# The first image normed within the attention, loads and output tail moved, and a reordered MLP, in an attention and Fourier mixer kernel

## The chip, the cores and the metric

The kernel runs on one core of a Trainium2 chip. The core has a matrix engine (TensorE, PE in the profile; its weight loads are PEld), three engines for elementwise work (VectorE or DVE, ScalarE or ACT, GpSimd or POOL), a sync engine (SP) that issues DMAs here, and 16 DMA engines. Each engine works through its own instructions in order, so an instruction that waits holds up all behind it on that engine. The metric is device time in microseconds (us); lower is better. Since there is one core, its span is the time, but for a little around it.

## What is computed

Eight images of 128 x 128 positions and 64 channels, float32, go through two layers. The first is an attention of every position over its own column (H) and its own row (W), with one softmax over both. The second is a Fourier mixer block: layer norm, expansion to 128 channels, a 2D Fourier transform, a matrix over real and imaginary parts with GELU, the inverse transform, projection back; then a convolutional MLP. Cut to what matters:

```python
def _L0_conv_ref(x, w_q, b_q, w_k, b_k, w_v, b_v, gamma):
    ...
    att = jax.nn.softmax(jnp.concatenate([energy_H, energy_W], axis=-1), axis=-1)
    att_H, att_W = (att[..., :H], att[..., H:])
    out_H = jnp.einsum('bhwk,bkwc->bhwc', att_H, V)
    out_W = jnp.einsum('bhwv,bhvc->bhwc', att_W, V)
    return gamma[0] * (out_H + out_W) + x
...
    h = _pw(_ln(x, g1, b1), w_te, b_te)
    F = jnp.fft.fft2(h.astype(jnp.complex64), axes=(1, 2))
    fr = jnp.concatenate([jnp.real(F), jnp.imag(F)], axis=-1)
    fc = jax.nn.gelu(_pw(fr, w_fc, b_fc), approximate=False)
    re, im = (fc[..., :HID], fc[..., HID:])
    sp = jnp.real(jnp.fft.ifft2(re + 1j * im, axes=(1, 2)))
    x1 = x + _pw(sp, w_tp, b_tp)
    h2 = _pw(_ln(x1, g2, b2), w_fe, b_fe)
    d = lax.conv_general_dilated(h2, w_dw, window_strides=(1, 1), padding='SAME', dimension_numbers=('NHWC', 'HWIO', 'NHWC'), feature_group_count=HID) + b_dw
    d = jax.nn.gelu(d, approximate=False)
    return x1 + _pw(d, w_fp, b_fp)
```

## The kernel before

The program has two halves. All eight images pass the attention, whose result x2 is written to DRAM (one tensor for each image); then all eight pass the mixer, which reads x2 back.

**The attention** (lines 91 to 448) runs each image in 16 slots: n = 0 to 7 attend over H, n = 8 to 15 over W. The order on PE, DVE, ACT and POOL is the order of the code. A slot makes scores (e, L217), maxima (L226), exponentials (L258), for H a masking of the diagonal on POOL (L260), and the sums with the values. In the W slots from n = 10 on, and in two trailing slots, finish(o, r) makes an eighth of the output: POOL adds the bias to the input (xb, L327, twice), DVE forms the sum of the denominators (L336, from sumh, which was loaded back from DRAM) and scales (yo, L349), POOL adds both (yo, L354, twice), SP stores to x2 (L356), and DVE takes the statistics for the next layer norm (L366); after the last of them the reciprocal deviation goes to scale1. While an image is in its slots, the next one is loaded and transposed (xT, in a pool with one large buffer). During the last image's W slots there is no next image.

**The mixer** (lines 451 to 965) first prepares its constants (weights folded with norms, the tables of the transform), then takes one image after the other. Only PE's order is that of the code here. DVE, ACT, POOL and SP are ordered by a scheduler, which goes by its own estimate of when each instruction can run.

- load_norm(b), L576 to L600, reads x2 in 16 chunks of four row pairs (h, 128 - h): one DMA of 128 KB (L584) and four of 32 KB (L587), a multiplication by the deviation (L588), sum and difference of the pair into xn (L593, L594). The first chunk has a copy (L596) and a small matmul for row 64 (qp, L598). DVE does this for image 0, POOL for the others.
- fourier(b), L605 to L703, has three stages. W: 256 matmuls over one axis (aps, L614, copied by ACT at L615). K, the frequency stage: 19 steps, each with the other axis (fps, L630), the 256 x 256 matrix (fcps, L650), GELU (L655, ACT), sums on POOL (L658 to L668) and a projection (gps, L686). I: the inverse over both axes (yps, L708; dps, L717), and DVE adds the result to x1, which is two loaded halves of x2 (x, L722).
- mlp(b), L731 to L937, takes the finished x1 in 16 chunks of eight rows: statistics (L743, DVE), normed rows (xc, L750, POOL), transposition (tpn, L765 on PE; xtn, L768 on ACT; for some chunks row 0 of xtn is a copy on POOL, L762), and then either of two ways to the 3 x 3 convolution. Most chunks expand to 128 channels (hp, L789; h, L793) and take nine taps on ACT and DVE (acc, L839, L841), then GELU (L849). The chunks in on_pe (5 and 10; for the last image 1, 3, 5 to 13) do expansion and taps as matmuls (pc, L804, L808, L815). At the end POOL adds the bias to x1 (ot, L859), PE shrinks to 64 channels (op, L864), DVE adds (L868), SP stores (L869). tpn, hp, pc and op share two PSUM buffers; ot has two buffers as well. An iteration (k, e) of the loop handles a chunk k with taps and, in some of the iterations, a chunk e with matmuls; the order of the e iteration is: transpositions, convolved(e), expand of the next k, shrink.

The main loop (L947 to L965) weaves mlp(b - 1) into fourier(b): mlp is cut into 79 pieces by its yields, and after each step of fourier as many pieces are issued as keep their share at 1.04 times the share of fourier's work that is done (weights: W 1.0 a step, K 6.3, I 1.8). load_norm(b + 1) is taken into the I stage. After fourier(b) the remaining pieces are issued, and only then the next image. After image 7 its mlp runs alone.

Some of the lines:

```python
                    while share < 1.04 * pieces * done / work:
                        next(before, None)
                        share += 1
                    if step == I_STEP and done > work - I_STEP * 18.5:
                        next(after, None)
```

## Time and profile before

| | |
|---|---|
| median of 4 runs | 3625.1 us (3609.41 to 3628.69) |
| the profiled execution | 3609.96 us, span 3608.2 us |
| mean granted clock of TensorE | 0.905 of full |
| end of the attention's last addition (L354) | 1279.6 us |
| first matmul of image 0 in the mixer (L614) | 1349.7 us |
| first L614 of images 1 to 7 | 1531.8, 1797.8, 2071.5, 2335.3, 2608.0, 2879.4, 3150.5 us |
| last dps (L717) of image 7 | 3406.9 us |
| image 0: W, K, I stage | 18.2, 115.6, 48.4 us (no MLP beside it) |
| image 4: W, K, I stage | 19.6, 194.6, 58.4 us |

The stages' lengths are the distances between the first matmuls of L614, L630 and L708. A window of the trace gives for each engine its busy time in that stretch with its number of instructions, then TensorE's mean granted clock, the mean busy share of the DMA engines, and GB/s. A group has the line of the code, the engine, the operation, its operands and shape, its count, then busy time, the mean of one in ns, and the idle time just ahead of such instructions with what ended it. The chain of waits follows the work that ended last: start, length, what; "issue" is a stretch in which nothing on the engine explains the wait, and SPq and POOLq are the queues of SP and POOL. In the slices each digit is the busy share of a fortieth of the span in tenths.

### The profile page before, as it was taken

To read this page: it belongs to the slowest core of one execution; us is meant where nothing else is said; L and a number is where in the kernel's file an instruction comes from. 1 tells how busy PE (TensorE), PEld (TensorE's weight loads), DVE (VectorE), ACT (ScalarE), POOL (GpSimd) and SP (SyncE) were. 2 spreads that over 40 slices of the span, in tenths; PEclk is the share of its full clock that TensorE was granted. 3 is DMA by queue.
4 is the path that set the end of the run, shared out by engine and by line. 5 is a ranking of instruction groups with operands and counts; after the bars stand their busy time and mean duration, and the time that the engine had idled before them with its cause. 6 is when DMAs were issued, how large, how long until landed. Compare 5 with 4: busy or idle time off the path is not lost.

```text
span 3608.2 us, 77249 instructions
## 1 busy us (share of the span) xinstructions
PE 3176.5 (88%) x30612; PEld 2185.1 (61%) x30612; DVE 2293.7 (64%) x5373; ACT 1781.9 (49%) x2861; POOL 1815.7 (50%) x2148
## 2 busy tenths in 40 slices
PE   7989899898998929799899899799899799899697
PEld 4666666666666716566656556556656556656455
DVE  3565565756657560266776776776776776776865
ACT  3535445354453306365465476465465365466332
POOL 0233332433324416856755766756756755756221
PEclk8989999999999859899898899998899898999886
DMA  4434344353443250101301301301301301301011
GB/s 107 125 87 126 91 127 117 102 130 103 120 112 99 75 163 1 44 13 44 89 9 44 86 11 45 89 12 41 89 12 42 89 9 44 83 12 45 16 21 27
DMA packets 579068, 243.66 MB, mean 68 GB/s; under 512 B 490770, under 2 KB 576146, under 8 KB 576658
## 3 DMA queue, kind: packets, MB, share of 16 engines
q1 hardware_dynamic: 578706, 238.72, 25.5%
q8 instruction: 242, 3.96, 0.5%
q14 instruction: 120, 0.98, 0.1%
HBM read 169.92 MB, written 67.63 MB: 66 GB/s over the span
## 4 chain that ended last, share of the span: by engine, by line
PE 47%; ACT 8%; DVE 6%; POOL 5%; issue 4%; DMA 3%; SPq 2%; POOLq 0%; ACTq 0%; DVEq 0%
PE fcps L650 11%; PE gps L686 6%; PE op L864 6%; PE hp L789 4%; PE pc L804 3%; PE fps L630 3%; DMA xl<-x 2%; PE e L217 2%; DVE acc L841 2%; SPq L587 2%; PE pc L815 2%; DVE stats L743 2%; PE aps L614 2%; ACT gl L655 1%; PE dps L717 1%
## 5 line engine op out<-in xcount | busy, mean ns | idle before, releaser
L841 DVE SCALAR_TENSOR_TENSOR acc<-h,wdw,acc 128x512 f32<-128x512 f32 (+2 forms) x1776 | 1194.1, 730 | 207.2 <-ACT acc L839 194.3
L658 POOL TENSOR_TENSOR gl<-gl 128x512 f32<-128x512 f32 (+2 forms) x272 | 332.0, 1224 | 370.5 <-ACT gl L655 369.7
L655 ACT ACTIVATE gl<-fcps,bfc 128x512 f32<-128x512 f32 (+2 forms) x544 | 359.7, 672 | 122.4 <-PE fcps L650 106.7
L354 POOL TENSOR_TENSOR yo<-yo,xb 128x512 f32<-128x512 f32 x128 | 161.1, 1280 | 422.4 <-issue 272.4
L258 ACT ACTIVATE att<-e 128x1024 f32<-128x1024 f32 x256 | 248.3, 1022 | 240.6 <-PE e L217 240.5
L864 PEld LDWEIGHTS op<-wfp,gd 128*128 128x128 f32 x2048 | 284.2, 219 | 124.9 <-ACT gd L849 53.2
L864 PE MATMUL op<-wfp,gd 128*128 128x64 f32 x2048 | 293.0, 303 | 71.4 <-ACT gd L849 50.1
L260 POOL TENSOR_SCALAR_AFFINE_SELECT att<-att 128x1024 f32<-128x1024 f32 x128 | 136.9, 1094 | 400.1 <-ACT att L258 400.1
L868 DVE TENSOR_TENSOR ot<-op,ot 128x512 f32<-128x512 f32 (+2 forms) x136 | 89.5, 658 | 364.1 <-PE op L864 216.4
L650 PE MATMUL fcps<-f,wplus 128*128 128x512 f32 (+2 forms) x544 | 292.9, 621 | 26.7 <-ACT gl L655 25.6
L650 PE MATMUL fcps<-f,wminus 128*128 128x512 f32 (+2 forms) x544 | 280.3, 597 | 1.7 <-ACT gl L655 1.7
L686 PEld LDWEIGHTS gps<-wtp,gl 128*128 128x128 f32 x2016 | 255.8, 205 | 29.5 <-issue 21.0
L686 PE MATMUL gps<-wtp,gl 128*128 128x64 f32 x2016 | 264.5, 288 | 1.9 <-POOL gl L668 1.9
L859 POOL TENSOR_TENSOR ot<-x,bfp 128x512 f32<-128x512 f32 (+2 forms) x144 | 164.9, 1151 | 162.8 <-DMA out_dram<-ot 136.0
L217 PE MATMUL e<-qkH 8*128 8x128 f32 (+1 forms) x4096 | 196.4, 310 | 54.0 <-DVE negH L226 50.1
L217 PEld LDWEIGHTS e<-qkH 8*128 8x128 f32 (+1 forms) x4096 | 160.2, 207 | 117.8 <-DVE negH L226 60.5
L217 PEld LDWEIGHTS e<-qkW 8*128 8x128 f32 (+1 forms) x4096 | 138.8, 191 | 125.1 <-DVE negW L226 37.2
L722 DVE TENSOR_TENSOR x<-dps,x 128x256 f32<-128x256 f32 x256 | 100.7, 416 | 174.9 <-PE dps L717 174.5
L750 POOL TENSOR_TENSOR xc<-x,scale 128x512 f32<-128x512 f32 x128 | 132.5, 1045 | 148.2 <-PE tpn L765 106.0
L717 PE MATMUL dps<-ys,tb 128*128 128x512 f32 x256 | 152.2, 686 | 58.7 <-DVE x L722 58.0
L226 DVE TENSOR_REDUCE negH<-e 128x8 f32<-128x1024 f32 x128 | 149.9, 1213 | 78.7 <-PE e L217 78.7
L217 PE MATMUL e<-qkW 8*128 8x128 f32 (+1 forms) x4096 | 169.0, 290 | 27.4 <-DVE negH L226 17.4
(167 smaller groups left out, 6198.1 us busy)
## 6 DMA issues: line engine op xcount, KB each, us to landing
xl<-in_x_dram SPq DMA_DIRECT2D x256, 128.0 KB
xh<-in_x_dram SPq DMA_DIRECT2D x64, 512.0 KB
xw<-in_x_dram SPq DMA_DIRECT2D x256, 128.0 KB
x<-yo SPq DMA_DIRECT2D x256, 128.0 KB
x<-x SPq DMA_DIRECT2D x16, 2048.0 KB
out_dram<-ot SPq DMA_DIRECT2D x120, 256.0 KB
xl<-x SPq DMA_DIRECT2D x128, 128.0 KB
xl<-x SPq DMA_DIRECT2D x512, 32.0 KB
```

The costliest lines, as they stand in the source:

```text
L217: nc.tensor.matmul(es[q // 2][:, q % 2, i, :], lhsT=qk[part, lhs, 4 * (r % 2) + i, :], rhs=qk[part, rhs, 4 * (r % 2) + i, :], start=True, ...
L226: nc.vector.tensor_reduce(view[:, 2 * g : 2 * g + 2, 4 * r : 4 * r + 4], e, AX.X, ALU.max, negate=True)
L258: nc.scalar.activation(att, e.rearrange("p q i w -> p (q i) w"), AF.Exp)
L354: nc.gpsimd.tensor_tensor(flat, flat, xbs[g], ALU.add)
L650: nc.tensor.matmul(ps[:, 0:n], lhsT=w[:, cols], rhs=fv, start=True, stop=not mean)
L655: nc.scalar.activation(gl[:, half, sgn, 0:n], ps[:, 0:n], AF.Gelu, bias=bfc[:, half : half + 1])
L658: nc.gpsimd.tensor_tensor(gl[:, half, 1, 0:n], gl[:, half, 0, 0:n], gl[:, half, 1, 0:n], ALU.add if half == 0 else ALU.subtract,)
L686: nc.tensor.matmul(gps[:, j, t, :], lhsT=src[:, j * P : j * P + P], rhs=wtp, start=True, stop=True)
L717: nc.tensor.matmul(dps.rearrange("p c h -> p (c h)"), lhsT=idw, rhs=ys.rearrange("p c h -> p (c h)"), start=True, stop=True)
L841: nc.vector.scalar_tensor_tensor(out=av, in0=src, scalar=wdw[:, t : t + 1], in1=av, op0=ALU.mult, op1=ALU.add)
L859: nc.gpsimd.tensor_tensor(ot[:, o : o + m, :], rows, bfp.unsqueeze(1).to_broadcast([P, m, C]), ALU.add)
L864: nc.tensor.matmul(op[:, i, :], lhsT=gls[k][:, i0 + a + i, :], rhs=wfp, start=True, stop=True)
```

## The change

Six edits. (1) Image 0 is loaded, scaled and folded beside the last image's attention: in each of its W slots SP issues the loads of eight row pairs (one of 256 KB and eight of 32 KB) and POOL does the scaling, the sum and the difference, at the end of the slot, into a buffer that outlives the attention; the row for the small matmul is kept, and the matmul stands at the mixer's end of preparation. (2) The large buffers of the mixer alternate between this outer pool and its own, one each instead of two in one pool. (3) The two x1 halves are requested at steps 10 and 17 of K rather than after K. (4) The factor 1.04 becomes 1.0; what is left of an MLP after its image's fourier is carried into the next image's steps, one piece after every fourth, and the end of the MLP is cut into more pieces. (5) In iterations with an e, expand stands ahead of convolved. (6) The MLP after the last image takes the statistics of 24 rows, the first norming, then those of the other 40.

```diff
+X1_AT = (10, 17)
...
+def folded(eng, xl, xn, scale, j):
+    n = xl.shape[2]
+    eng.tensor_tensor(xl, xl, scale[:, :, j : j + n].unsqueeze(3).to_broadcast([P, 2, n, C]), ALU.mult)
+    i = 0 if j else 1
+    one, two = (xl[:, s, i:, :].rearrange("p h c -> p c h") for s in range(2))
+    eng.tensor_tensor(xn[:, :, j + i : j + n], one, two, ALU.add)
+    eng.tensor_tensor(xn[:, :, 64 + j + i : 64 + j + n], one, two, ALU.subtract)
+    if j == 0:
+        eng.tensor_copy(xn[:, :, 0], xl[:, 0, 0, :])
+def load_pairs(nc, xl, img, j):
+    n = xl.shape[2]
+    nc.sync.dma_start(out=xl[:, 0, :, :], in_=img[:, j : j + n, :])
+    for i in range(n):
+        h = P - j - i if j + i else 64
+        nc.sync.dma_start(out=xl[:, 1, i, :], in_=img[:, h, :])
...
-                o.xT = big.tile([P, 64, P], F32, tag="xt", name="xt")
+                o.xT = one.tile([P, 64, P], F32, tag="xt", name="xt")
...
+            if cur and not nxt and n >= R:
+                j = 8 * (n - R)
+                if n == R:
+                    cur.xn = one.tile([P, C, P], F32, tag="xt", name="xn")
+                pairs = rows.tile([P, 2, 8, C], F32, tag="xl", name="xl", bufs=2)
+                load_pairs(nc, pairs, x2[0], j)
+                folded(nc.gpsimd, pairs, cur.xn, scale1[:, 0, :].rearrange("p (s j) -> p s j", s=2), j)
+                if j == 0:
+                    nc.gpsimd.tensor_copy(row64, pairs[:, 1, 0, :])
...
-        big = ctx.enter_context(tc.tile_pool(name="m_big", bufs=2))
+        big = ctx.enter_context(tc.tile_pool(name="m_big", bufs=1))
...
-        images = {}
+        images = {0: {"xn": xn0}}
+        turns = iter([big, first] * (2 * NB))
+        def large(shape, name):
+            return next(turns).tile(shape, F32, tag="xt", name=name)
+        def quarter_shifted(xn, row):
+            qp = ps_m.tile([P, C], F32, tag="mm", name="qp")
+            nc.tensor.matmul(qp, lhsT=quarter, rhs=row, start=True, stop=True)
+            nc.scalar.copy(xn[:, :, 64], qp)
         def load_norm(b):
-            xn = big.tile([P, C, P], F32, tag="big", name="xn")
+            xn = large([P, C, P], "xn")
             images[b] = {"xn": xn}
             scale = scale1[:, b, :].rearrange("p (s j) -> p s j", s=2)
-            eng = nc.gpsimd if b else nc.vector
             for j in range(0, 64, PAIRS):
                 xl = p2.tile([P, 2, PAIRS, C], F32, tag="xl", name="xl")
-                nc.sync.dma_start(out=xl[:, 0, :, :], in_=x2[b][:, j : j + PAIRS, :])
-                for i in range(PAIRS):
-                    h = P - j - i if j + i else 64
-                    nc.sync.dma_start(out=xl[:, 1, i, :], in_=x2[b][:, h, :])
-                eng.tensor_tensor(
-                    xl, xl, scale[:, :, j : j + PAIRS].unsqueeze(3).to_broadcast([P, 2, PAIRS, C]), ALU.mult
-                )
-                i = 0 if j else 1
-                one, two = (xl[:, s, i:, :].rearrange("p h c -> p c h") for s in range(2))
-                eng.tensor_tensor(xn[:, :, j + i : j + PAIRS], one, two, ALU.add)
-                eng.tensor_tensor(xn[:, :, 64 + j + i : 64 + j + PAIRS], one, two, ALU.subtract)
+                load_pairs(nc, xl, x2[b], j)
+                folded(nc.gpsimd, xl, xn, scale, j)
                 if j == 0:
-                    eng.tensor_copy(xn[:, :, 0], xl[:, 0, 0, :])
-                    qp = ps_m.tile([P, C], F32, tag="mm", name="qp")
-                    nc.tensor.matmul(qp, lhsT=quarter, rhs=xl[:, 1, 0, :], start=True, stop=True)
-                    nc.scalar.copy(xn[:, :, 64], qp)
+                    quarter_shifted(xn, xl[:, 1, 0, :])
...
-            at = big.tile([P, P, C], F32, tag="big", name="at")
+            at = large([P, P, C], "at")
...
-            gt = big.tile([P, C, 2, 64], F32, tag="big", name="gt")
+            gt = large([P, C, 2, 64], "gt")
...
+            xs = im["x1"] = []
+            for n_g, g in enumerate(groups + [None, None]):
+                if n_g in X1_AT:
+                    s = len(xs)
+                    xs.append(xp.tile([P, 64, C], F32, tag="x1", name="x1"))
+                    nc.sync.dma_start(out=xs[s], in_=x2[b][:, 64 * s : 64 * s + 64, :])
...
-            xs = im["x1"] = []
-            for s in range(2):
-                xt = xp.tile([P, 64, C], F32, tag="x1", name="x1")
-                nc.sync.dma_start(out=xt, in_=x2[b][:, 64 * s : 64 * s + 64, :])
-                xs.append(xt)
...
-                if hi == 64:
-                    deviation(nc, p2, sts[s], epsc, scale[:, 64 * s : 64 * s + 64])
+                if done is not None:
+                    deviation(nc, p2, sts[s][:, done:hi, :], epsc, scale[:, 64 * s + done : 64 * s + hi])
...
-            statistics(0, 0, 64)
-            normed(0)
-            for k in ready(0):
+                    hi = n * (i - first) + n
+                    statistics(1, hi - n, hi, 0 if hi == 64 else None)
+            now = [0] + ready(0)
+            if b + 1 < NB:
+                statistics(0, 0, 64, 0)
+            else:
+                statistics(0, 0, 24, 0)
+            for k in now:
                 normed(k)
+            if b + 1 == NB:
+                statistics(0, 24, 64, 24)
...
                 if e:
+                    for c in after:
+                        expand(c)
                     convolved(e)
                 yield
-                for c in after:
-                    expand(c)
+                if not e:
+                    for c in after:
+                        expand(c)
...
             gelu(n_ch - 1, 1)
             taps(n_ch - 1, 2, 0, 9)
+            yield
             gelu(n_ch - 1, 2)
-            for a in (0, CH):
-                store(*shrink(n_ch - 1, a))
+            held = shrink(n_ch - 1, 0)
+            yield
+            store(*held)
+            store(*shrink(n_ch - 1, CH))
...
+        quarter_shifted(xn0, row64)
...
-        for _ in load_norm(0):
-            pass
+        carried = iter(())
         for b in range(NB + 1):
             before = mlp(b - 1) if b > 0 else iter(())
             after = load_norm(b + 1) if b + 1 < NB else iter(())
             if b < NB:
                 done, share = 0.0, 0
-                for step in fourier(b):
+                for n, step in enumerate(fourier(b)):
                     done += step
-                    while share < 1.04 * pieces * done / work:
+                    if n % 4 == 3:
+                        next(carried, None)
+                    while share < pieces * done / work:
                         next(before, None)
                         share += 1
-                    if step == I_STEP and done > work - I_STEP * 18.5:
+                    if done > work - I_STEP * 18.5:
                         next(after, None)
-            for rest in (before, after):
+            for rest in (carried, after):
                 for _ in rest:
                     pass
+            carried = before
+        for _ in carried:
+            pass
```

In the order that results on PE, a frequency stage that had, for a chunk e, `pc x14, hp x4, gps x8` has `hp x4, pc x14`, followed by gps or fcps; at the end of an image the first eight matmuls of op of chunk 15 stand after the last dps and before the first L614, its last one among them. On DVE 46 long and 2 short taps stand between the first and the last x addition of images 1 to 7, where 34 long and 8 short ones stood. On SP the loads of x1 stand nearly where they were.

## The prediction

> **What bounds the kernel now.** I read the page's busy row and slices first, then the windows around the hole they show, the chain of waits there, the groups of POOL by shape, and the stages of the second half one by one (a stage runs from the first matmul of L614, L630 or L708 to the next).
>
> ```profile
> PE 3176.5 (88%) x30612; PEld 2185.1 (61%) x30612; DVE 2293.7 (64%) x5373; ACT 1781.9 (49%) x2861; POOL 1815.7 (50%) x2148
> ...
> PE   7989899898998929799899899799899799899697
> ...
> POOL 0233332433324416856755766756756755756221
> PEclk8989999999999859899898899998899898999886
> ```
>
> TensorE is the bound nearly everywhere; its slice 15 holds a 2 and the last slices fall off. So time can come from holes on TensorE, from its clock, or from its instructions, and the change removes no matmul. The windows across the hole (the columns are PE, PEld, DVE, ACT, POOL, clock, DMA share, GB/s):
>
> ```profile
> 1221.00:1280.00 59.00, 54.02 (x790) 42.34 (x786) 41.83 (x175) 21.87 (x26) 39.98 (x33) 1.00 0.39 108
> 1300.00:1340.00 40.00, 0.00 (x0) 0.00 (x0) 20.13 (x33) 0.00 (x0) 0.00 (x0) 0.50 0.62 203
> ```
>
> Ahead of the hole POOL has 19 of 59 us free while TensorE is full; in it only DVE and the DMAs work: it is load_norm(0), 16 chunks of four row pairs. The chain of waits gives its two edges:
>
> ```profile
> 1278.36 1.27 POOL yo L354
> ...
> 1298.77 50.92 issue
> 1349.69 0.66 PE aps L614 x2
> ```
>
> The frequency stages (L630 to the last L686) of images 2 and 3, as windows:
>
> ```profile
> 1817.40:2012.10 194.70, 184.42 (x904) 119.69 (x905) 129.63 (x193) 118.75 (x205) 123.71 (x165) 0.92 0.12 30
> 2091.10:2275.80 184.70, 174.52 (x916) 113.13 (x917) 131.14 (x195) 118.81 (x206) 125.09 (x168) 0.98 0.13 32
> ```
>
> Same work, ten microseconds apart, and only the granted clock differs. Images 1 to 7 take 187.7, 194.7, 184.7, 194.6, 191.1, 196.1 and 184.4 at 0.96, 0.92, 0.98, 0.93, 0.95, 0.92, 0.98: mean 190.5 at 0.949, and 0.06 of clock is worth 11 us. The end of an image, as the chain has it for image 2:
>
> ```profile
> 2064.19 0.02 SPq L869
> 2064.24 2.60 DMA out_dram<-ot
> 2066.98 0.32 POOL ot L859
> 2067.33 0.23 DVE ot L868
> 2067.55 0.67 DVE x L722 x2
> 2068.36 3.24 PE dps L717 x4
> ```
>
> An output store stood on SP behind the next image's loads; with two ot buffers POOL waits for it, DVE's add waits for POOL (8.0 us idle before that add), and the last x additions wait behind it. Last, the MLP that runs alone after image 7 (3406.9 to 3608.2):
>
> ```profile
> 3440.00:3580.00 140.00, 126.61 (x481) 78.58 (x480) 76.91 (x116) 45.61 (x81) 30.45 (x58) 0.78 0.12 25
> 3580.00:3608.00 28.00, 12.24 (x50) 11.12 (x50) 21.87 (x38) 5.22 (x9) 1.98 (x3) 0.50 0.15 30
> ```
>
> TensorE is again the bound, at 0.78 of its clock, and in the last 28 us DVE's taps.
>
> **What the Trainium skill says.** "TensorE: Matmul & The Clock Gate", Part 1 (What's actually happening): the array runs at half clock after an idle window of about 3.4 us and is released by a busy one. The trace agrees: 0.50 in the hole, and half-clock stretches elsewhere of 6.8, 10.2 and 13.7 us, multiples of 3.4. "GPSIMD Engine Reference", 4.1 Engine selection: two-input elementwise work is about twice as slow there as on VectorE. The trace shows 1.5 to 1.6: L588 of 128x512 took 0.70 us on DVE and 1.04 on POOL, L593 of 128x256 took 0.67 and 1.08. The trace decides. "DMA: Bandwidth & Descriptors", Issuing engines are not separate DMA queues: all transfers share 16 engines, so the moved loads compete with the attention's. No run here shows both together.
>
> **Part 1, image 0 normed in the last eight W slots.** It removes the DVE work of 1297.3 to 1350.2 and adds to each slot 9 loads on SP and one fold of eight pairs on POOL. POOL's rows by shape:
>
> ```profile
> L354 POOL TENSOR_TENSOR yo<-yo,xb 128x512 f32<-128x512 f32 x128 | 161.1, 1280 | 422.4 <-issue 272.4 <-DMA qkH<-joint 79.4 <-DMA xh<-in_x_dram 22.6
> L327 POOL TENSOR_TENSOR xb<-xw,bv 128x512 f32<-128x512 f32 x128 | 160.6, 1278 | 0.0
> L588 POOL TENSOR_TENSOR xl<-xl,scale 128x512 f32<-128x512 f32 x112 | 116.8, 1043 | 136.6 <-DMA xl<-x 134.8 <-issue 1.5
> L593 POOL TENSOR_TENSOR xn<-xl 128x256 f32<-128x256 f32 x105 | 112.9, 1075 | 7.1
> L594 POOL TENSOR_TENSOR xn<-xl 128x192 f32<-128x192 f32 x7 | 6.0, 854 | 0.0
> ```
>
> 256 against 192 elements differ by 0.22 us, so 512 take 1.08 + 4 x 0.22 = 1.96 us; the scaling of 1024 takes about 1.9. A fold is 1.9 + 2 x 1.96 = 5.8 us, eight are 47 (with two copies of 0.3). The attention's own finish is 2 x 1.28 + 2 x 1.28 = 5.1 us in each of eight slots, 40 in all. POOL's last select of the H slots ends at 1221.2; 1221.2 + 47 + 40 = 1308 against 1279.6, so POOL becomes the bound and the attention ends 28.7 later. If POOL's waits interleave badly or the loads are late, one slot in two may lose 2 us (+8); if the long shapes cost less than in proportion, 5.1 instead of 5.8, -6. The loads: 9 issues of 0.43 us are 4 us of SP in a slot that now lasts 10.9; 0.39 x 6.4 + 0.62 x 6.6 = 6.6 us of DMA time also fits. SP's sumh loads (L336 waits for them) stand behind them, about +1, hidden as POOL is late anyway. After the attention the preparation of constants (1279.6 to 1292.4, 12.8 us) follows as before, then the quarter matmul and its copy, 1.2: first L614 at 1322.3 instead of 1349.7. **-27 us** (-35 to -17). The hole is 57 us, half of it is given back.
>
> **Part 2, pieces at 1.0 instead of 1.04, tail carried.** Of 79 pieces the frequency stage gets 59 before, 56 after (W is 16, K 119.7 and I 32.4 of 168.1 units). Image 0's stage, without pieces, takes 115.6; the others 75 more for 59, 1.27 each: three cost -3.8. They go to the I stage, where TensorE is busy 46 of 59 us. There the order on DVE decides: between the first and the last x addition stood 34 long and 8 short taps, 32 additions, 3 output adds, 34 x 0.75 + 8 x 0.35 + 32 x 0.415 + 3 x 0.69 = 44 us, plus the stall of 8 and waits: 53. Now 46 long and 2 short taps stand there, 51 us, and the 128x64 output add is moved past them into W. The stall goes and DVE fills its place: The stage, 57.6 in the mean, becomes about 55, **-2.5 us** for each of images 1 to 6 (-6 to +3; next late is POOL's norming of the next image, 16 x 3.2 = 51 us). Image 7 has little of the stall (52.4): **+3**. The tail adds 0.3 us to each W (17.9 us of L614 in 19.6): **+2** in all. The 4 us of loads, x1 halves at K steps 10 and 17: SP's order leaves both nearly where they were, 0; no wait in K comes from them.
>
> **Part 3, expand ahead of TensorE's convolution.** In K the light run pc (64 rows), hp, gps becomes hp, pc, op: hp's few columns now stand ahead of a dense block. In the trace of before, seven of the half-clock stretches in K begin right after pc, hp, gps, four after hp, op, gps, op. I take half of the loss away: clock 0.949 to 0.975, -5 us an image (0 to -9). With -3.8 of pieces and some of it lost to waits, **-8 us** in each of seven K stages, -56. Against it: hp now needs row 0 of its input from POOL's copy (0.30 us, L762), behind whatever POOL does, with 12 pc matmuls queued behind it on TensorE; the trace shows no such wait, bounds 0 to 2 us, twice an image; taken inside the 8.
>
> **Part 4, last MLP.** Statistics in 24 rows first: the stage begins with 64 of them,
>
> ```profile
> 3407.69 8.12 DVE stats L743 x64
> ```
>
> 40 x 0.127 = **-5 us**. With expand ahead, each of seven periods (18.1 us warm, 24.2 with 13.7 at half clock) waits for the copy, about 1 us: **+6** (-15 if the clock holds, +20 if it is half throughout).
>
> Sum: -27 - 15 + 3 + 2 - 56 - 5 + 6 = -92. The profiled execution took 3609.96 (span 3608.2) and would take 3518; the median of the four runs is 3625.1, so I forecast 3625 - 92 = **3533 us**.
>
> **Rivals.** (a) The clock doesn't change: K gains 3.8 each only, last MLP +10: -27 - 15 + 3 + 2 - 27 - 5 + 10 = -59, 3566. For it: the triggers depend on where a free-running window falls, and 0.92 and 0.98 alternate in equal code. (b) The clock holds in K (0.99) and in the last MLP: -27 - 15 + 5 - 80 - 20 = -137, 3488. For it: seven of the triggers share the one pattern that goes. (c) Slower: hp's wait for the copy starves TensorE of work just before the dense block, and half-clock stretches begin there every time. The place is the two such iterations of each K stage and the seven of the last MLP; a stretch is 13.7 us long and costs half, 6.8. With two of these and the old 8 us of others K falls from 0.949 to about 0.89, -3.8 + 11 = +7 an image, +49, and the last MLP, three quarters of it at half clock, loses 35: -27 - 15 + 3 + 2 + 49 - 5 + 35 = +42, 3667. It decides below a K clock of about 0.915. For it: the light runs are where stretches begin now, and hp is the lightest. Against it: the dense block follows at once. (d) The start gains nothing, because a fold takes 9.2 us beside the attention's own traffic (8 x 3.4 = 27): -92 + 27 = -65, 3560. (e) The 7 us of extra taps don't fill the stall but come on top of it, because x additions queue behind them and dps behind those, and chunk 15's output matmuls, which the new order puts ahead of and among the next image's L614, wait 2 us for the same taps: 9 lost instead of 2.5 won, 6 x 11.5 = 69, so -23, 3602.
>
> **Chances.** Forecast 0.42, (a) 0.2, (b) 0.12, (d) 0.1, (e) 0.08, (c) 0.08. Own range of the forecast 3505 to 3555; the range that takes in (a), (d) and most of (b) is 3478 to 3588. A run can't tell less than 0.5% (18 us) from nothing; (e) stands at that edge and gives half of its chance to no change: faster 0.87, same 0.05, slower 0.08.
>
> **What would show it.** Slots of the last W half at about 10.9 us with POOL full, first L614 near 1322; hole of TensorE about 14 us, not 57; K stages at 183 and 0.975; no 8 us idle before the 128x64 output add; I near 55 with DVE full; tpn of the last MLP 5 us earlier after the last dps. Wrong if POOL's eight-pair fold isn't near 5.8, if K's clock is still 0.95, or if I passes 60.

## The result, and the profile after

The changed kernel took 3594.9 us (median of 37 runs) where the kernel before took 3628.5 (median of 56): 0.9924 of it, interval 0.9908 to 0.9939, some 28 us less. The ratio leaves out executions more than 1.5% above the fastest of the same kernel, so it is not the quotient of the two medians. I had forecast 92 us less, 3533, and the time lies above the wide range, 3478 to 3588.

The profiled executions, 3608.2 and 3597.3 us of span, differ by 11 us. Cut at the same matmuls, this is where the two differ. "Masking" is POOL's last selection in the H slots (L260 before, L282 after); W, K and I are means over images 1 to 7; the last MLP runs from the last dps to the last instruction of an engine, about 3 us ahead of the span's end. The second profile of the changed kernel is the first of the experiments.

| us | before | after | after, second profile |
|---|---|---|---|
| start to last masking (code unchanged) | 1221.2 | 1247.7 | 1250.8 |
| last masking to first aps | 128.5 | 99.4 | 99.5 |
| W | 19.9 | 24.8 | 24.8 |
| K | 190.7 | 191.1 | 191.3 |
| I | 57.2 | 51.4 | 50.9 |
| last MLP | 198.3 | 193.4 | 198.0 |

The page of after, with the rows that answer to those shown of before:

```profile
PE 3191.3 (89%) x30612; PEld 2191.5 (61%) x30612; DVE 2267.8 (63%) x5329; ACT 1785.0 (50%) x2864; POOL 1860.5 (52%) x2174
...
PE   7989999998989969789899899889889889899787
...
POOL 0233333424333386865765765765765765765321
PEclk8989898988999779899899899899899899899878
```

The 2 of TensorE's slice 15 has become a 6, and POOL's slice 15, a 1 before, is now an 8. So the hole is mostly closed: POOL does this work beside the attention, as meant. But the total busy time of TensorE rose by 15 us for the same matmuls, and the clock's row is no higher than before where the MLP runs beside K. Windows of after, first the stretch from the last masking to the attention's end and the preparation behind it, then W, K and I of image 4 (columns: PE, PEld, DVE, ACT, POOL busy, clock, DMA share, GB/s):

```profile
1247.70:1333.80 86.10, 64.34 (x782) 50.72 (x778) 41.74 (x172) 21.87 (x26) 85.36 (x59) 0.84 0.41 111
1333.80:1347.10 13.30, 5.72 (x18) 2.99 (x18) 7.20 (x33) 0.40 (x1) 1.23 (x11) 0.50 0.54 125
2335.30:2362.70 27.40, 21.63 (x267) 18.79 (x267) 21.31 (x139) 13.52 (x24) 9.80 (x12) 0.83 0.35 109
2362.70:2552.90 190.20, 173.90 (x896) 112.30 (x897) 127.13 (x188) 114.70 (x198) 124.38 (x165) 0.95 0.12 30
2552.90:2604.80 51.90, 43.27 (x238) 31.57 (x237) 46.59 (x93) 22.66 (x40) 41.27 (x47) 0.93 0.34 82
```

POOL is busy for 85.4 of the 86.1 us: it is the bound there, and the 86 us are close to the 87 that the prediction had for folds and finishes. One fold and one finish on POOL's timeline (start, length, operation):

```profile
1264.49 1.91 POOL L96 TENSOR_TENSOR xl<-xl,scale 128x1024 f32<-128x1024 f32 x1
1266.47 2.00 POOL L99 TENSOR_TENSOR xn<-xl 128x512 f32<-128x512 f32 x1
1268.41 2.01 POOL L100 TENSOR_TENSOR xn<-xl 128x512 f32<-128x512 f32 x1
1270.36 2.52 POOL L349 TENSOR_TENSOR xb<-xw,bv 128x512 f32<-128x512 f32 x2
1272.82 2.51 POOL L376 TENSOR_TENSOR yo<-yo,xb 128x512 f32<-128x512 f32 x2
```

K holds 20 matmuls fewer than before (896 against 916) and still isn't shorter. On TensorE's timeline of that stage two waits stand out, and POOL's timeline says what the first is waiting for:

```profile
2489.29 1.11 PE L665 MATMUL fps<-tb,at 128*128 128x128 f32 x8
2494.28 0.49 PE L820 MATMUL hp<-xtn,wfe 64*128 64x128 f32 x4 [3.89 <-POOL xtn L793]
2495.23 2.33 PE L820 MATMUL hp<-xtn,wfe 64*128 64x512 f32 x4 [0.45 <-ACT h L824]
...
2540.97 2.04 PE L721 MATMUL gps<-wtp,gl 128*128 128x64 f32 x12 [2.43 <-POOL gl L703]
```

```profile
2486.77 1.28 POOL L890 TENSOR_TENSOR ot<-x,bfp 128x512 f32<-128x512 f32 x1
2488.01 1.04 POOL L781 TENSOR_TENSOR xc<-x,scale 128x512 f32<-128x512 f32 x1
2489.01 1.28 POOL L693 TENSOR_TENSOR gl<-gl 128x512 f32<-128x512 f32 x1
2490.25 1.04 POOL L781 TENSOR_TENSOR xc<-x,scale 128x512 f32<-128x512 f32 x1
2491.23 0.21 POOL L699 COPY gl<-gl 128x16 f32<-128x16 f32 x1
2491.39 1.25 POOL L700 TENSOR_TENSOR gl<-gl 128x504 f32<-128x504 f32 x1
2492.61 1.39 POOL L703 TENSOR_TENSOR gl<-gl 128x252 f32<-128x252 f32 x2
2493.95 0.28 POOL L793 COPY xtn<-xtn 128x128 f32<-128x128 f32 x1
```

The copy takes 0.28 us. It was late because it stands in POOL's order behind the seven lines above it (eight operations), and hp, since it went ahead of the convolution, waits for it with everything behind it. The same wait of 3.9 us stands once in each of the seven K stages. Beside it the clock goes to half, for 6.8 us in this stage and 6.8 to 10.2 in the others: the second hp line, 2.33 us for four matmuls, takes 1.38 in a version with the wait gone and the clock full (tail_old, shown with the experiments).

The other wait, of gps, is 2.43 us in this stage and 2.0 to 2.4 in images 1 to 6. POOL has put the next image's scaling ahead of the sums that gps needs, and that scaling waits for its load:

```profile
2538.24 1.04 POOL L96 TENSOR_TENSOR xl<-xl,scale 128x512 f32<-128x512 f32 x1 [2.28 <-DMA xl<-x]
...
2540.32 1.13 POOL L703 TENSOR_TENSOR gl<-gl 128x189 f32<-128x189 f32 x2
```

Beside this wait 13.7 to 17.1 us at half clock begin. Image 7, which has no next image, has neither.

For W the lines are, on SP, POOL and TensorE in turn:

```profile
2343.88 0.32 SPq L654 DMA_DIRECT2D x<-x  x1
2344.29 1.01 SPq L900 DMA_DIRECT2D out_dram<-ot  x2
```

```profile
2352.68 1.13 POOL L890 TENSOR_TENSOR ot<-x,bfp 128x448 f32<-128x448 f32 x1 [8.74 <-DMA out_dram<-ot]
2353.77 4.05 POOL L781 TENSOR_TENSOR xc<-x,scale 128x512 f32<-128x512 f32 x4
```

```profile
2354.87 1.12 PE L796 MATMUL tpn<-m_ident,xc 128*128 128x128 f32 x4 [2.79 <-POOL xc L781]
```

The stall that stood at the end of I is now in W: the carried output add runs behind 59 statistics on DVE, so its store is issued after 2 MB of x1, lands 8.3 us later, and POOL's two ot buffers hold up the norming, the transposition and L644 behind it. The clock has a part in W too: in images 2 to 7 TensorE waits 2.5 us for the GELU ahead of the carried op matmuls, and about a microsecond later, just ahead of the first L644, a stretch of 6.8 us at half clock begins. In the mean W has 7.2 us at half clock, 1.1 before.

### The profile page after: what moved, and what is told of

The parts are those of the page before. It is cut to its first block, busy times and chain, and to the rows that moved or that the text cites. A ratio compares the mean times of both kernels' runs of the same rounds, so it can differ in the third digit from the quotient of the medians.

```text
span 3597.3 us, 77151 instructions
## 1 busy us (share of the span) xinstructions
PE 3191.3 (89%) x30612; PEld 2191.5 (61%) x30612; DVE 2267.8 (63%) x5329; ACT 1785.0 (50%) x2864; POOL 1860.5 (52%) x2174
## 4 chain that ended last, share of the span: by engine, by line
PE 61%; DVE 13%; POOL 8%; ACT 8%; issue 5%; DMA 3%; SPq 2%; POOLq 0%; DVEq 0%; ACTq 0%
PE fcps L685 10%; PE e L239 7%; PE op L895 5%; PE gps L721 5%; DVE acc L872 5%; PE pc L835 4%; PE zp L302 4%; PE hp L820 3%; PE sp L326 3%; PE pq L220 3%; PE fps L665 3%; PE zp L315 3%; DVE negH L248 2%; POOL yo L376 2%; PE tp L199 2%
## 5 line engine op out<-in xcount | busy, mean ns | idle before, releaser
L282 POOL TENSOR_SCALAR_AFFINE_SELECT att<-att 128x1024 f32<-128x1024 f32 x128 | 136.9, 1095 | 420.0 <-ACT att L280 420.0
L895 PEld LDWEIGHTS op<-wfp,gd 128*128 128x128 f32 x2048 | 261.5, 203 | 135.1 <-ACT h L824 61.5
L895 PE MATMUL op<-wfp,gd 128*128 128x64 f32 x2048 | 269.6, 287 | 72.4 <-ACT gd L880 35.5
L685 PE MATMUL fcps<-f,wminus 128*128 128x512 f32 (+2 forms) x544 | 272.0, 582 | 1.1 <-ACT gl L690 1.1
L721 PEld LDWEIGHTS gps<-wtp,gl 128*128 128x128 f32 x2016 | 244.1, 197 | 39.4 <-POOL gl L703 16.8
L721 PE MATMUL gps<-wtp,gl 128*128 128x64 f32 x2016 | 253.5, 280 | 14.9 <-POOL gl L703 14.5
L239 PEld LDWEIGHTS e<-qkH 8*128 8x128 f32 (+1 forms) x4096 | 167.6, 215 | 119.4 <-DVE negH L248 57.1
L824 ACT ACTIVATE h<-hp,bfe 128x512 f32<-128x512 f32 (+1 forms) x256 | 150.5, 635 | 115.3 <-PE hp L820 115.2
L332 ACT COPY ss<-sp 128x512 f32<-128x512 f32 x128 | 75.1, 587 | 266.2 <-PE sp L326 204.8
L820 PE MATMUL hp<-xtn,wfe 64*128 64x512 f32 (+1 forms) x512 | 160.2, 674 | 47.4 <-POOL xtn L793 31.9
```

The costliest lines, as they stand in the source:

```text
L239: nc.tensor.matmul(es[q // 2][:, q % 2, i, :], lhsT=qk[part, lhs, 4 * (r % 2) + i, :], rhs=qk[part, rhs, 4 * (r % 2) + i, :], start=True, ...
L685: nc.tensor.matmul(ps[:, 0:n], lhsT=w[:, cols], rhs=fv, start=True, stop=not mean)
L721: nc.tensor.matmul(gps[:, j, t, :], lhsT=src[:, j * P : j * P + P], rhs=wtp, start=True, stop=True)
L820: nc.tensor.matmul(hps[s], lhsT=wfe[half, :], rhs=xt[half, j : j + n, 1 : P + 1], start=True, stop=True)
L895: nc.tensor.matmul(op[:, i, :], lhsT=gls[k][:, i0 + a + i, :], rhs=wfp, start=True, stop=True)
```

## The experiments

Means over images 1 to 7, in us; "mixer" is from the first aps to the last instruction. All but the named edits are as in the changed kernel, unless it says "before with". Each ratio is to executions of the kernel before made beside that run (medians 3615 to 3636 us).

| run | what it is | ratio to before | interval | W | K | I | last MLP | mixer |
|---|---|---|---|---|---|---|---|---|
| before | | 1 | | 19.9 | 190.7 | 57.2 | 198.3 | 2255.5 |
| after_again | the change | 0.9916 | 0.9883 to 0.9950 | 24.8 | 191.3 | 50.9 | 198.0 | 2251.2 |
| first_only | before with the norming | 0.9931 | 0.9901 to 0.9961 | 19.9 | 189.9 | 57.1 | 198.4 | 2250.7 |
| expand_only | before with expand ahead | 0.9833 | 0.9792 to 0.9874 | 19.9 | 184.2 | 57.1 | 185.5 | 2196.9 |
| expand_late | expand behind | 0.9779 | 0.9729 to 0.9830 | 22.0 | 189.7 | 50.6 | 211.5 | 2231.3 |
| tail_old | factor and tail of before | 0.9710 | 0.9666 to 0.9755 | 19.9 | 183.7 | 57.0 | 182.5 | 2190.2 |
| factor_104 | factor of before | 0.9734 | 0.9692 to 0.9775 | 21.0 | 183.1 | 53.9 | 187.2 | 2175.9 |
| factor_100 | tail of before, factor 1.0 | 0.9950 | 0.9930 to 0.9970 | 21.2 | 191.4 | 56.7 | 186.5 | 2254.7 |
| copy_act | L793 on ACT | 0.9774 | 0.9739 to 0.9809 | 25.7 | 183.8 | 51.4 | 188.4 | 2198.3 |
| ot3 | three ot buffers | 0.9878 | 0.9836 to 0.9920 | 22.5 | 192.2 | 50.9 | 193.4 | 2237.7 |
| tail_old_ot3 | tail_old, three ot buffers | 0.9696 | 0.9652 to 0.9741 | 19.7 | 182.0 | 54.3 | 180.3 | 2157.5 |
| best3 | tail_old_ot3, L793 on ACT | 0.9703 | 0.9659 to 0.9747 | 19.7 | 182.1 | 54.2 | 183.0 | 2160.0 |
| early | expand_late, folds earlier | 0.9861 | 0.9822 to 0.9899 | 22.4 | 188.9 | 50.7 | 211.3 | 2230.3 |
| best | early, three ot buffers | 0.9860 | 0.9796 to 0.9924 | 22.3 | 186.2 | 51.3 | 211.4 | 2216.4 |
| best2 | tail_old_ot3, folds split | 0.9701 | 0.9661 to 0.9742 | 19.7 | 182.1 | 54.7 | 182.5 | 2163.5 |

**The same kernel again.** No edit.

> The changed kernel once more, for a second profile. Its attention up to the last H slot is the code of before, but its last masking (L282) ended at 1247.7 us where before's ended at 1221.2. If that is TensorE's clock, which falls otherwise in every execution, it ends elsewhere now, between 1210 and 1250, while the stretch from there to the first L644 stays at 99 us, and so do W near 25 and I near 52. If the change itself slows the attention (its outer pool, its loads), it is 1245 to 1250 again. Time 0.990 to 0.994 of before.

The last masking ended at 1250.8 us, as in the first profile; the ratio was 0.9916. By these two alone the 26 us ahead of the masking look like the change's own. The other runs speak against it: with the same attention code up to there, the masking ended at 1228.6 (expand_late), 1229.8 (first_only), 1229.9 (tail_old), 1232.0, 1234.7, 1238.1, 1246.0, 1247.1, 1251.6 and 1253.9 (expand_only, whose attention is that of before to the last line). TensorE's time at half clock up to the masking went with it, from 205 us (before, the earliest of all) to 297 (expand_only). No edit orders these, so I don't count the attention's clock as an effect of the change; whether it falls by execution or goes with the program isn't settled, since only one program was profiled twice. That the clock of the whole does fall differently by execution can be seen in best below: its six executions took 3552 to 3608 us, at mean clocks of 0.910 to 0.893. What follows is that the profile of before has the earliest masking of all, and that parts are to be compared from the first aps on.

**Image 0's norming alone.** To the kernel before are added folded, load_pairs, the two pools and the fold in the last W slots, with everything else as it was, but that the first load of the next image's norming is taken one step earlier, at the end of K, as in the changed kernel (the condition on I_STEP is gone there, which the six edits don't name):

```diff
+            if cur and not nxt and n >= R:
...
+                load_pairs(nc, pairs, x2[0], j)
+                folded(nc.gpsimd, pairs, cur.xn, scale1[:, 0, :].rearrange("p (s j) -> p s j", s=2), j)
...
-        for _ in load_norm(0):
-            pass
```

> Of the change only image 0's norming beside the attention, with the two pools: loads, factor, tail, expand and statistics as before. From the last masking of the attention to the first L644 it takes 99 us instead of 128.5 (-29); W, K and I of images 1 to 7 as before (20, 190, 57). The whole is 0.992 of before, about what the whole change gives. Rival, that POOL's folds also slow what comes before them, or that the time comes back later: 0.997 or more.

From masking to first aps it takes 99.2 us, W, K and I are those of before within a microsecond (so the earlier load costs nothing here), and the ratio is 0.9931, 25 us (14 to 36). This part of the prediction holds.

**Expand behind convolved, and expand ahead alone.** The first takes the order back in the changed kernel, the second puts it into the kernel before:

```diff
                 if e:
-                    for c in after:
-                        expand(c)
                     convolved(e)
                 yield
-                if not e:
-                    for c in after:
-                        expand(c)
+                for c in after:
+                    expand(c)
```

> The changed kernel with expand behind convolved again, all else kept. My prediction had this order worth 5 us of clock in each K stage: then K rises from 191 to about 196 and the whole to 1.0 of before. What I think now: the half-clock stretches only move, K stays within 3 us of 191 in the mean, hp's waits for ACT and POOL shrink by some 2 us an image, and the last MLP moves by less than 8 us; the whole 0.987 to 0.995.

It was neither: 0.9779, about 50 us better than the change, with K only 1.6 shorter, W 2.8 shorter and the last MLP 13 to 18 longer. The profile of this run had its masking 20 us earlier too, so that the gap can't be put down to the edit as a whole; the mixer is 16 to 20 us shorter, and where the rest of the 50 lies isn't shown.

> The kernel before with expand ahead of convolved alone. The changed kernel lost 50 us against its own version without this order. If that price lies in TensorE's new waits (idle in K 15.9 us with it, 11.5 without), K's idle goes from 10.3 to about 15, K gets 2 to 4 us longer apiece, W and I stay at 20 and 57, the last MLP within 8 us of 198, and the whole is 1.003 to 1.009 of before. If the order costs as much here as there, 1.012 to 1.016. If my prediction's step was right, the clock in K rises and the whole is 0.99.

Both prices that I expected were wrong, and the prediction's own step, which I had given up, was right: K falls from 190.7 to 184.2, at a mean clock of 0.98 instead of 0.95, and the last MLP from 198.3 to 185.5. The window of K of image 4 in this run:

```profile
2373.40:2554.70 181.30, 171.47 (x916) 109.93 (x917) 131.67 (x195) 118.48 (x205) 124.91 (x168) 1.00 0.13 32
```

The matmuls are those of before, in the same stage, 13 us faster than the 194.6 of image 4 before, at a clock of 1.00 instead of 0.93. So the order is worth what the prediction hoped for in the old spacing of pieces, and does harm in the new one: 0.9833 against 1 there, 0.9916 against 0.9779 here, with the reservation above.

**The factor and the tail, taken apart.** tail_old takes both back, factor_104 the factor alone, factor_100 the tail alone:

```diff
-                    while share < pieces * done / work:
+                    while share < 1.04 * pieces * done / work:
...
-            for rest in (carried, after):
+            for rest in (before, after):
                 for _ in rest:
                     pass
-            carried = before
```

> The changed kernel with factor 1.04 again, the MLP issued to its end within its own image and its tail uncut; all else kept, expand ahead too. If the shorter I stages (52 against 58) and the longer W stages (24.8 against 19.9) both come from the carried tail, I returns to 56 to 59 and W to about 20, K rises by about 3 (three pieces more), and the whole is 0.995 to 1.002 of before. Rival, that I is shorter by the x1 loads within K or by the expand order: I stays at 52.

W and I return as expected, and K doesn't rise by 3 but falls by 7: the whole is 0.9710, a larger gain than any above.

> The changed kernel with the factor 1.04 alone taken back; the cut tail and the carrying stay in the code. If the factor is what spoils the change, because it moves each of the MLP's pieces to another step of K (after the convolution's matmuls then come gps and op instead of fps and fcps), K falls from 191 to 183 to 186, its idle from 15.9 to about 10 and the last MLP to 180 to 187; the whole is within 0.4% of 0.971. If the carried tail is what spoils it, K and the whole stay near the changed kernel's 191 and 0.992.

> The changed kernel with the tail uncut and the rest of each MLP issued within its own image, but at factor 1.0. If the factor spoils K: K about 190 with idle near 16, W about 20, the whole 0.985 to 0.995 of before. If the carried tail does: K 184 and the whole 0.971 to 0.976.

The factor is it. With 1.04 K is 183.1 and the whole 0.9734, with 1.0 and no carrying K is 191.4 and the whole 0.9950. The windows of K of image 4, factor_104 and factor_100:

```profile
2312.00:2495.00 183.00, 173.16 (x917) 110.47 (x917) 131.73 (x196) 118.44 (x205) 125.02 (x168) 0.99 0.13 32
```

```profile
2355.70:2547.80 192.10, 175.50 (x897) 113.58 (x897) 126.87 (x188) 114.56 (x198) 124.15 (x165) 0.94 0.12 29
```

The second does 20 matmuls fewer in 9 us more. Busy time is the same or higher at the lower clock, and TensorE's idle time is 16.6 against 9.8 us.

**Which wait the factor makes.** At factor 1.04, in tail_old, the same hp stands behind eight matmuls of the frequency stage (fcps), and POOL's copy ends before TensorE gets there (POOL, then TensorE):

```profile
2442.72 0.30 POOL L793 COPY xtn<-xtn 128x128 f32<-128x128 f32 x1
```

```profile
2444.38 0.49 PE L820 MATMUL hp<-xtn,wfe 64*128 64x128 f32 x4
2445.48 1.38 PE L820 MATMUL hp<-xtn,wfe 64*128 64x512 f32 x4 [0.61 <-ACT h L824]
```

To see what the wait costs, the copy alone is taken off POOL in the changed kernel, with TensorE's order unchanged to the last matmul:

```diff
-                nc.gpsimd.tensor_copy(xt[:, 0, 1 : P + 1], xts[k - 1][:, 4, 1 : P + 1])
+                nc.scalar.copy(xt[:, 0, 1 : P + 1], xts[k - 1][:, 4, 1 : P + 1])
```

> The changed kernel with the copy of row 0 of the transposed chunk (L793) on ACT instead of POOL; TensorE's order is the same to the last matmul. At factor 1.0 hp waits 3.9 us in each K stage for this copy, which stands behind seven POOL operations, and a half-clock stretch of 6.8 us begins there. If that wait is what the factor costs, the gap goes, K's idle falls from 15.9 to 12 and K from 191 to 185 or less, the whole to 0.980 to 0.985 of before. If it is one cause among several (gps behind load_norm on POOL, gps and op after the convolution), idle falls as far but the half-clock stretches move elsewhere: K 187 to 190, the whole 0.985 to 0.990. If the copy is innocent: 0.992.

K falls from 191 to 183.8, TensorE's idle time in it from 15.7 to 11.9 in the mean, the last MLP to 188.4 and the whole to 0.9774, about 50 us better than the change. K of image 4:

```profile
2344.70:2527.60 182.90, 170.80 (x896) 111.15 (x897) 127.16 (x188) 115.06 (x202) 123.31 (x161) 0.97 0.12 31
```

One 0.28 us copy on another engine gives seven microseconds in each of seven stages: TensorE's idle time falls by 3.8 and its time at half clock from 22.0 to 12.2, worth up to half of the difference, 4.9. W doesn't gain by it (25.7).

It isn't all that the factor costs. The wait of gps stays, about 2 us in images 1 to 6, and 13.7 to 17.1 us at half clock begin there as before. At factor 1.04 no gps waits a microsecond, and K is as short, 183.1 in factor_104, with 20 matmuls more. No run takes this second wait away alone.

Where hp stands behind more work the same edit is worth nothing:

> The version with the old factor and tail and three ot buffers, and that copy on ACT. There hp waits under a microsecond, so I expect no more than 1 us an image: 0.965 to 0.971 of before.

0.9703 against 0.9696 without it. As expected, since POOL's copy was in time there.

**Three ot buffers.** The small matmul's row is kept in xn's own place to make room:

```diff
-                ot = p2.tile([P, CH, C], F32, tag="ot", name="ot")
+                ot = p2.tile([P, CH, C], F32, tag="ot", name="ot", bufs=3)
...
-                    nc.gpsimd.tensor_copy(row64, pairs[:, 1, 0, :])
+                    nc.gpsimd.tensor_copy(cur.xn[:, :, 64], pairs[:, 1, 0, :])
```

> Three ot buffers instead of two (the row for the small matmul is kept inside xn, which frees the room). If the longer W stages (24.8 us in the mean of images 1 to 7, 19.9 before) come from POOL's bias addition, which waits 8.7 us for the output store behind a 2 MB load and holds up the norming, the first transposition and L644, W falls to about 20 with the clock near 1.00, and the whole to about 0.984 of before (-30 us against the changed kernel). Rival, that W suffers from the carried matmuls and their half-clock stretches: W stays above 23 and the whole at 0.99.

Half right. W fell from 24.8 to 22.5, the whole to 0.9878, whose interval overlaps the change's. The wait for the store goes in most images; what is left over 19.9 goes with half-clock time in W, 4.9 us in the mean in this run. In images 2 to 7 it begins 0.5 to 1.4 us after TensorE's wait for the GELU ahead of the carried op matmuls, as in the changed kernel.

> The version with the old factor and tail, and three ot buffers. At the end of images 1 to 6 POOL waits for the store of two chunks earlier, and with it the last x additions (8 us on DVE in the kernel before). With a third buffer that goes: I from 57 to 51 to 53, the mixer (first L644 to the end) from 2190 to 2155 to 2170, the whole 0.960 to 0.966 of before. Rival, that DVE's taps take the place of the stall: I stays above 55.

I falls from 57.0 to 54.3, half of what I expected: the stall goes and DVE's taps probably keep part of its place. The mixer, 2157.5 us, is the shortest of all runs. The time, 3504 us or 0.9696, is above the 0.960 to 0.966 that I expected and isn't told apart from tail_old's 0.9710.

**Folds earlier.** early and best have this edit; best2 has `(4 <= n < 8 or n >= 12)` in its place, with j counted accordingly:

```diff
-            if cur and not nxt and n >= R:
-                j = 8 * (n - R)
-                if n == R:
+            if cur and not nxt and 4 <= n < 12:
+                j = 8 * (n - 4)
+                if n == 4:
```

> The changed kernel with expand behind convolved and the eight folds four slots earlier (slots 4 to 11 of the last image instead of 8 to 15). POOL has 7 of 9 us free in an H slot, so four folds of 5.9 us come out of the packed stretch: from the last masking to the first L644 76 us instead of 99, the masking itself later by 0 to 8. The whole 0.971 to 0.975 of before, where expand behind convolved alone gave 0.978. Rival, that folds delay the maskings and these TensorE: the masking later by 20 us and no gain.

> As early, with three ot buffers as well. W falls from 22 to 20 or 21 in images 1 to 7, -7 to -14 us: the whole 0.967 to 0.972 of before. Rival, that W at 22 is the clock's and not the store's: no difference to early.

> As tail_old_ot3, with four folds in the slots 4 to 7 of the last image and four in its slots 12 to 15, so that no fold stands behind SP's loads of the query and key rows (L271) and none ahead of the first finish. From the last masking to the first L644 78 to 84 us instead of 99: the whole 0.954 to 0.962 of before. Rival, that the early folds delay the maskings by as much: no difference to tail_old_ot3.

All three missed. From masking to first aps it took 102.3, 102.3 and 93.7 us instead of 76, 76 and 78 to 84. In best's POOL timeline the fifth fold, and with it all finishes behind it, waited for its rows:

```profile
1244.89 1.91 POOL L96 TENSOR_TENSOR xl<-xl,scale 128x1024 f32<-128x1024 f32 x1 [9.63 <-DMA xl<-x]
```

and the chain of waits there names SP, with 15 and more issues of L271 (the rows of queries and keys) of 0.63 us each ahead of the pair loads:

```profile
1232.09 1.49 SPq L271
1233.63 0.63 SPq L271
1234.30 0.63 SPq L271
1234.97 0.63 SPq L271
...
1238.89 0.44 SPq L110
```

I had counted POOL's time and left out SP's queue. The split of best2 avoids that, and then the finishes wait for DVE's scaling (8.07 us once); it gains 5.5 us of the 15 to 21 expected. early (0.9861) is also slower than expand_late (0.9779); its profile had a masking at 1249.9 and best's at 1229.3, so that this difference can't be told from the attention's clock. Between early and best the rival holds: W is 22.4 and 22.3, and the ratios are the same.

**Not tried:** the x1 loads alone and the statistics alone. tail_old has both and expand_only neither, with the same matmul order in the mixer: W, K and I agree within half a microsecond, so the x1 loads are worth nothing by themselves, as forecast. TensorE's wait ahead of the first tpn of the last MLP was 13.3 us before and is 7.9 in tail_old: the statistics' 5 us are there.

## Why the prediction was wrong

Part 1 was right. Forecast -27 from one fold at 5.8 us and one finish at 5.1; the rows are 5.9 and 5.0, POOL was the bound for 86 us, masking to first aps is 29 us shorter, and the part alone measured 25 (14 to 36).

Part 3 is the step that failed, in the term that it took "inside the 8". It forecast -8 us for each K stage, -56 in all, and K came out no shorter (191.1 against 190.7). The prediction named the wait (hp needs POOL's copy "behind whatever POOL does", with the convolution queued behind it on TensorE) and bounded it at 0 to 2 us since the trace of before didn't show it. It is 3.9 us in each of the seven stages, and 6.8 to 10.2 us of half clock begin beside it. That is most of the 8 us by which K is off: with the copy on ACT K is 7.3 us shorter, seven of these are 51, and about 50 us of the whole came back. The trace of before couldn't show the wait, since hp stood behind the convolution there. A better bound needed POOL's order around the copy, not the copy's duration: eight operations of 0.2 to 1.3 us stood ahead of it, and operations like them were in the rows of before.

The rest of the step was right: with the wait absent, the order takes K from 190.7 to 184.2, clock included, where I forecast 5 us for the clock and 0 to 9 as its bounds. Rival (c) had this very mechanism, hp's wait and a half-clock stretch behind it, and gave it 0.08; it was priced for both such iterations of each K stage and at 35 us for the last MLP. It came in one of the two, and in the last MLP, where hp waits 1.5 us twice, not as a loss.

Part 2 made the two meet. The factor wasn't a matter of three pieces, -3.8: it moves every piece to another fourier step, and with it what stands next to what on all engines. It put hp ahead of POOL's copy, and gps behind a norming that waits for its load, a wait of 2.0 to 2.4 us that the prediction doesn't name. K's -3.8 is in factor_100's count of matmuls and nowhere in its time.

The other sums of Part 2 were half right: I fell by 5.8 instead of the 2.5 forecast (image 7 by 5.4, where I had +3). That the whole still came out ahead owes much to this, 40 us where I had 12, and not to what I had counted on. But W, put at +0.3, rose by 4.9. About half of it is the store: the carried tail's output add went behind the statistics on DVE, and its store behind the x1 load, and a third buffer takes 2.3 us back. The other half goes with half-clock time that begins near the carried op matmuls; rival (e) had said that these would wait 2 us, and they wait 2.5. I had looked at what the tail adds to W and not at who waits for its store, although the same wait was the one I had just removed from I.

Part 4: the statistics gave 5 us. Expand ahead in the last MLP, forecast at +6, gives -13 (198.3 to 185.5 in expand_only), with 76 us at half clock instead of 109. Some of that is lost again in the changed kernel (193.4 and 198.0), whose carried tail of image 7 now runs after the last dps; how the loss divides between this tail and the clock isn't shown.

Two readings of before were loose. The K windows of images 2 and 3 don't end at the same matmul (904 against 916 instructions); cut alike, the stages hold 916 each and take 196.2 and 184.6. And the I stage is 57.2 us in the mean, not 57.6. Neither moves a term by a microsecond.

Added up as measured: -29, W +34, K +3, I -40, last MLP -5 to 0, is -32 to -37 from the masking on, at or just beyond the far end of the 22 to 33 us that the ratio's interval allows.

A version that beats both kernels is tail_old_ot3, 3504 us, 3.0% under before: the norming in the attention, expand ahead, split statistics, the old factor and tail, and three ot buffers. best2, best3, tail_old and factor_104 are not distinguishable from it.

## What to carry to other kernels

Where an instruction is moved ahead, ask for its latest input not how long the producer takes but what stands ahead of it on the producer's own queue, and bound the wait by the sum of those durations and of what those instructions wait for themselves. A pacing factor in a woven schedule isn't a small knob: a change of 4% moved each piece past other work and turned a gain of nearly 3% into one of 0.5 to 0.8%, so it is to be tried at several values with each edit of the order. And where a stall is moved rather than removed (two buffers and a store), look for it at the next consumer.

## What the runs showed of the hardware that was not expected

The Trainium skill's "TensorE: Matmul & The Clock Gate", Part 1, has the clock fall after an idle window of about 3.4 us. Here it fell beside the one wait of 3.9 us in K, in all seven stages, which fits. But it fell beside waits of 2.0 to 2.4 us as well, in six stages. And in K of before, where the prediction said that the trace agrees, all 13 half-clock stretches (6.8 to 13.7 us long) began with TensorE idle for at most 1.4 of the 4 us ahead; eleven of them came right behind runs of hp, op and gps, whose matmuls have 64 rows or 64 columns. That these light matmuls are the cause isn't shown. The same order of matmuls ran at 0.92 to 1.00 of the clock, in K stages of 196.1 to 181.7 us of one execution (first_only). The same attention code took 1221 to 1254 us up to the last masking, with 205 to 297 us of it at half clock, which is more than the whole change brought.
